# A convolution and a gated scan on one core: the last step's state kept as four plain blocks, the last block's z kept as fp16 halves and summed on TensorE

## The chip, the cores and the metric

The kernel runs on one core of a Trainium2 chip. A core has TensorE (PE in the profile: matmuls from SBUF into PSUM), VectorE (DVE), ScalarE (ACT), GpSimd (POOL) and SyncE (SP), which here issues every DMA of the scan from one queue, in order. The metric is the time of one execution on the device in microseconds, lower is better. An instruction waits on semaphores for what it needs; each engine runs its own instructions in the order in which the program lists them.

## The reference

Input r is 8 sequences of 2048 rows of 512 numbers. Two layers follow each other, both with a residual sum:

```python
x = r
x = x + LN(gelu(irfft(rfft(LN(x)) * Kf)))         # a long convolution over the 2048 rows, its kernel K made from S4 parameters
# second layer: x has shape (8, 2048, 512); axis 0 is the time of the recurrence, 2048 is its batch
c = broadcast(in_c)
for xt in LN(x):                                   # 8 steps
    f = sigmoid(xt @ wf.T + c @ uf.T + bf)
    i = sigmoid(xt @ wi.T + c @ ui.T + bi)
    g = tanh(xt @ wc.T + c @ uc.T + bc)
    c = f * c + i * g
h = tanh(LN(x) @ wo.T + c_final @ uo.T + bo)       # for every step, with the last state
out = x + LN(h)
```

So an output row of any step can only be finished when the last state c_final of its batch row is known.

## The kernel before, in words

**Stages.** The first 690 us or so compute the set-up and the convolution. From there to about 2790 us runs the scan, and the last 80 us finish output rows. The 2048 batch rows are worked in four blocks q of 512 (`NQB` = 4), each of four chunks of 128 rows (`QC` = 4); for every block the eight steps t are run one after the other (`NB` = 8), 32 steps in all, about 66 us each. Matrix products are made with fp16 pairs: a number is a high half plus a low half, and a product takes three matmuls (hi x hi, lo x hi, hi x lo; `mm3`). All values under a tanh or sigmoid are scaled by `SW` on the way.

**A step.** It has eight units: two z units (z0, z1: the part LN(x) @ wo.T of the output, for half of the block's rows each) and six gate units g0 to g5 (three gates, two halves). A unit multiplies 2 x 2 blocks by seven products in place of eight, so its operands are seven combinations of blocks (`xf`, `cf`, the weights). `part_a` issues the first products into a PSUM tile `u` (pool `pu`, three tiles that turn over), then ScalarE copies a quarter of it out (L988) and VectorE makes four additions (L989 to L992). `part_b` issues the remaining products; a gate unit then goes to ScalarE's tanh (L1016) and, with its unit's last gate, to `state`; a z unit is copied to SBUF by ScalarE (L1002, L1003, tile `zt`) beside the quarter `zc`, which VectorE's chain had made, and three DMAs store both to `z_d` in fp32.

On TensorE the units overlap: part_a of the next unit stands ahead of part_b of the one before. The start of a step is part_a(z0), the rest of the step before, part_a(z1), part_b(z0), part_a(g0), part_a(g1), part_b(z1), part_b(g0) and so on. With three tiles, g1 uses the tile of z0 and g2 that of z1.

**The state.** `state` makes the new c (`cd`, four blocks of 128 x 256) on VectorE, L1034 to L1037, three sums of blocks on VectorE (L1040 to L1042), and then `halves` splits seven blocks, the four plain and the three sums, into fp16 pairs `cf`: four ScalarE copies (L1049) and four VectorE subtractions (L1051). For the first half of the state, `halves` is run later.

**Other work in the scan** is placed by hand: `put(list of functions, base, positions)` files small pieces under a position (16 positions a step), and `go(p)` issues those of position p. The main ones are `turn` (LN and the seven combinations of the next step's x), `prep` (last pieces of the convolution's rows), and `head`: during block q the output rows of block q-1 are finished, one at a time; z is read from `z_d` (tile `zr`), GpSimd adds the state's part `ur` (L1123), ScalarE makes the tanh (L1126), VectorE the statistics (L462 to L465), GpSimd the power (L471) and the signs (L475, L476), ScalarE the norm (L1140), and GpSimd adds x (L1141).

**The state's part of the output**, c_final @ uo.T + bo, is made by `last(q)` at the boundary of a block: `load` (weights `uw`), `load_b` (the bias bo), and per chunk `sums` (matmuls L450 to L452 over blocks of `cf`, some of them the sums' blocks) and `out` (ScalarE copies the PSUM tile, GpSimd adds the bias, L1100), then `store` to `u_d`.

**The last block** has no block after it, so its 32 tiles of 128 x 512 (four chunks by eight steps) are finished behind the scan by `tail`, in 16 pairs of tiles; such a pair is called a row below. The first nine rows' z are loaded before the scan ends. A row goes through `load` (z from `z_d`), `load_x`, `sum_` (two VectorE adds of the state's part in PSUM, L1174, and two tanh on ScalarE, L1175), `stat` (VectorE and GpSimd), `norm` (ScalarE, L1182), `out` (x + norm: GpSimd, L1187, one in eight of them on VectorE) and `store` (L1190). A loop issues the stages of several rows interleaved, by offsets:

```python
for st_, d in ((0, -3), (1, -3), (6, 5), (2, 1), (3, 2), (4, 3), (5, 3)):
```

Nine z tiles and nine x tiles turn over, so that x of row n + 9 can be loaded when the store of row n has landed; SP's queue has both, in order.

Of the kernel before, what the change touches and what calls it, by code (L numbers as in the profile page):

```python
# [19 lines left out]
P = 128  # L20
L = 2048
H = 512
# [37 lines left out]
def s4_gated_block(ctx, tc, a, dbg=None):  # L60
# [10 lines left out]
    x1_d = dram.tile([NJ, P, NB, H], F32, name="x1_d")  # L71
    z_d = dram.tile([NJ, P, NB, H], F32, name="z_d")
    u_d = dram.tile([NJ, P, H], F32, name="u_d")
    wf_d = dram.tile([7, P, 2, 7, 2, BP], F16, name="wf_d")
# [379 lines left out]

    def lnstat(src, tag):

        n = len(src)
        st = FE.tile([P, n, 6], F32, name="st" + tag)
        mv = FE.tile([P, n, 2], F32, name="mv" + tag, bufs=2)
        rs = FE.tile([P, n], F32, name="rs" + tag, bufs=2)  # L460
        for i, v in enumerate(src):
            V.bn_stats(st[:, i], v)  # L462
        for i in range(n):
            V.bn_aggr(mv[:, i], st[:, i])
        V.tensor_scalar(rs, mv[:, :, 1], EPS, None, ALU.add)  # L465
        return n, mv, rs, tag
# [527 lines left out]
    def part_b(key):  # L994
# [3 lines left out]
        wx, wc = views(key)  # L998
        mms(u, places(key, THEN), *wx, False, z or not t)
        if z:  # L1000
            zt, zc = FT.tile([P, 3, BP], F32, name="zt"), gates["z"]
# [23 lines left out]
    def state(q, t, n):  # L1025
# [5 lines left out]
        for h in range(2):  # L1031
            hs = slice(2 * h, 2 * h + 2)
            if t == 0:
                V.tensor_scalar(f[:, hs], f[:, hs], 1.0, c0d[:, n + 2 * h : n + 2 * h + 1], ALU.add, ALU.mult)  # L1034
            else:
                V.scalar_tensor_tensor(f[:, hs], f[:, hs], 1.0, cd[:, hs], ALU.add, ALU.mult)  # L1036
            V.scalar_tensor_tensor(cd[:, hs], f[:, hs], 0.5, ig[:, hs], ALU.mult, ALU.add)  # L1037

        ts = f
# [17 lines left out]
    def last(q):  # L1057
# [14 lines left out]

        def load_b():
            bo = FE.tile([P, H], F32, name="bo", tag="xa", bufs=2) if end else FT.tile([P, H], F32, name="bo", tag="x1r", bufs=2)
            dma(out=bo, in_=a["bo"])
            uws.append(bo)

        def sums(cj):
# [5 lines left out]
            us[cj] = u  # L1084
            ps = [(k, b) for k in ((0, 2, 1, 3) if end else range(KT)) for b in (((FB11,) if i == 0 else (FB11, FT1)) if k < 2 else ((FB21,) if i == 0 else (FB22,)))]
            for n, (k, b) in enumerate(ps):
                mm3(u[:, cj % 2], lambda l: cf[k % 2][:, b, l, cs], lambda l: uws[k][:, l],
                    start=(n == 0), stop=(n == len(ps) - 1))

        def out(cj):  # L1090
            p_ = us[cj][:, cj % 2]
            if end:
                V.scalar_tensor_tensor(p_, uws[KT], SW, p_, ALU.mult, ALU.add)
                us_[QC * q + cj] = p_
            else:
                u_ = FT.tile([P, H], F32, name="u_", tag="zr", bufs=4)
                S.activation(u_, p_, AF.Copy)
                if cj == 0:
                    S.mul(uws[KT], uws[KT], SW)
                Q.tensor_tensor(u_, u_, uws[KT], ALU.add)  # L1100
                uo.append(u_)
# [6 lines left out]
        each = [one(f, cj) for cj in range(QC) for f in (sums, out)]  # L1108
        return [load, load_b] + (each[::2] + each[1::2] if end else each + [store])

# [37 lines left out]
    def tail(q, cj, tp, n):  # L1148
# [3 lines left out]
        def load():  # L1152
# [3 lines left out]
            s_["z"] = tails[w][:, n % 3]  # L1156
            dma(out=s_["z"], in_=z_d[c, :, 2 * tp : 2 * tp + 2])

# [12 lines left out]
        def sum_():  # L1171
            for i in range(2):
                z = s_["z"][:, i]
                V.tensor_tensor(z, z, us_[c], ALU.add)  # L1174
                S.activation(z, z, AF.Tanh, scale=1.0 / SW)  # L1175

        def stat():
            s_["s"] = lnscale(lnstat([s_["z"][:, i] for i in range(2)], "h"))

# [4 lines left out]
        def out():  # L1184
            for i in range(2):
                z, x = s_["z"][:, i], s_["x"][:, i]
                (V if n % 4 == 3 and i else Q).tensor_tensor(x, x, z, ALU.add)  # L1187

        def store():
            dma(out=a["out"][c, :, 2 * tp : 2 * tp + 2], in_=s_["x"])  # L1190

        return load, load_x, sum_, stat, norm, out, store

    tails = {}
    gsc = (0.5 / SW, 0.5 / SW, 1.0 / SW)
    bias = FE.tile([P, 3, KT], F32, name="bias")
# [26 lines left out]
    for n, (q, t) in enumerate(steps):  # L1223

        if n > 1 and t:
            when += [(n, p) for p in (at_(5, 10, 15) if t in (2, 3) or n == 4 else at_(5, 10) if t == NB - 1 else (PA, PB))]
    end = last(NQB - 1)
    rows = [tail(NQB - 1, cj, tp, 4 * cj + tp) for cj in range(QC) for tp in range(NB // 2)]

# [5 lines left out]
    for n, (q, t) in enumerate(steps):  # L1235
# [5 lines left out]
        if q and t == 0:  # L1241
            put(last(q - 1), b, (-1, 4, 3, 5, 5, 7, 7, 9, 13, 14, 15))
        if n == len(steps) - 1:
            put(end[:2], b, (2, 3))
            for i in range(3):
# [11 lines left out]
    with tc.manual_schedule(engines=MAN | {mybir.EngineType.SP}):  # L1257
# [25 lines left out]
        for p in sorted(todo):  # L1283
            go(p)
        for f in end[2:6]:
            f()
        for n in range(len(rows) + 5):
            if n % 4 == 0 and n < len(rows):
                end[6 + n // 4]()
            for st_, d in ((0, -3), (1, -3), (6, 5), (2, 1), (3, 2), (4, 3), (5, 3)):  # L1290
                if 0 <= n - d < len(rows) and (st_ > 1 or n - d > (2 if st_ else 8)):
                    rows[n - d][st_]()

_CONSTS = {}
# [60 lines left out]
```

## Time and profile before

| what | value |
|---|---|
| time, median of 3 runs | 2872.67 us (2871.69 to 2873.89) |
| the profiled execution: span from first to last instruction | 2869.6 us |
| what lies around the span (median less span) | 3.1 us |
| mean granted TensorE clock | 0.966 of full speed |
| TensorE / VectorE / ScalarE / GpSimd busy | 89% / 73% / 52% / 42% of the span |
| step length in the scan where nothing waits | 65.94 us |
| stretch from 2802 us to the end | 67.6 us: VectorE 57.0, GpSimd 54.0, ScalarE 42.0, TensorE 5.9 us busy |

How to read it: an answer of the trace has the start in microseconds, the duration, the engine, the line of the kernel and the operation with its tiles; a bracket tells how long the engine stood idle before it and what ended that. A group xN is N instructions in a row. Lines are those of the kernel before. The profile is of one execution; its times are compared with each other, and the sum of a prediction is carried over to the median with the 3.1 us.

### The profile page before, as it was taken

How to read it: one execution, taken by the hardware profiler on the slowest of the kernel's cores; microseconds unless marked ns; L12 is line 12 of the kernel's file. 1: busy time of each engine (PE TensorE's matmuls, PEld its weight loads, DVE VectorE, ACT ScalarE, POOL GpSimd, SP SyncE). 2: the span in 40 equal slices, each digit the busy share in tenths (PEclk: the TensorE clock that was granted, in tenths of full speed). 3: DMA queues.
4: the chain of work that ended last, by engine and by line, in shares of the span. 5: the costliest groups of instructions: out<-in, count | busy, mean ns of one | idle time of the engine just before them, and what ended most of it. 6: DMA issues, size and time to landing. Idle time of an engine off the chain costs nothing.

```text
span 2869.6 us, 60008 instructions
## 1 busy us (share of the span) xinstructions
PE 2567.3 (89%) x23940; PEld 2236.0 (78%) x23940; DVE 2097.3 (73%) x4248; ACT 1478.7 (52%) x3091; POOL 1213.1 (42%) x1496
## 2 busy tenths in 40 slices
PE   4588888876999999999999998999999999999991
PEld 3377777765888888778888886888888788888880
DVE  7878788837667766677777777777777677776758
ACT  8966666634344444445455544455454445544435
POOL 5776777613112221114554531355444124443317
PEclk8799999987999999999999999999999999999995
DMA  6978887797324333224565532355564235543356
GB/s 232 312 233 261 254 263 247 243 263 204 112 65 115 103 93 92 78 89 138 152 174 151 141 100 89 106 161 165 147 163 140 85 89 152 151 130 100 89 163 244
DMA packets 521937, 451.10 MB, mean 157 GB/s; under 512 B 289974, under 2 KB 401080, under 8 KB 516664
## 3 DMA queue, kind: packets, MB, share of 16 engines
q1 hardware_dynamic: 521224, 446.74, 52.4%
q8 instruction: 187, 3.06, 0.4%
q14 instruction: 94, 0.77, 0.1%
q10 hardware_dynamic: 432, 0.52, 0.1%
HBM read 295.41 MB, written 151.78 MB: 156 GB/s over the span
## 4 chain that ended last, share of the span: by engine, by line
PE 34%; DVE 9%; ACT 3%; DMA 2%; issue 1%; POOL 1%; SPq 0%; POOLq 0%; ACTq 0%; DVEq 0%
PE u L950 32%; PE pt L485 1%; DVE u L992 1%; DVE gate L1036 1%; DVE cf L1051 1%; DMA z_d<-zc 1%; ACT xf L101 1%; DVE cd L1037 1%; ACT gate L1016 1%; DVE sth L462 1%; DVE zz L1174 1%; DVE sty L462 1%; ACT y L903 0%; DVE u2p L989 0%; DVE xf L102 0%
## 5 line engine op out<-in xcount | busy, mean ns | idle before, releaser
L950 PEld LDWEIGHTS <-w 128*128 128x128 f16 x15120 | 1482.5, 98 | 217.2 <-issue 28.3
L950 PE MATMUL u<-xf,w 128*128 128x256 f16 x8064 | 947.6, 274 | 30.7 <-ACT zt L1003 12.7
L950 PE MATMUL u<-cf,w 128*128 128x256 f16 x7056 | 826.2, 273 | 3.8 <-DVE cf L1051 3.8
L988 ACT ACTIVATE u2p<-u 128x256 f32<-128x256 f32 x256 | 96.4, 378 | 449.8 <-PE u L950 449.6
L950 PE MATMUL u<-w,xf 128*128 128x256 f16 x2688 | 314.4, 275 | 14.8 <-DVE u L992 4.8
L989 DVE TENSOR_TENSOR u2p<-u2p,u 128x256 f32<-128x256 f32 x256 | 106.8, 417 | 285.8 <-ACT u2p L988 284.3
L1141 POOL TENSOR_TENSOR x1r<-x1r,zr 128x512 f32<-128x512 f32 x96 | 132.7, 1382 | 426.8 <-ACT zr L1140 309.4
L1016 ACT ACTIVATE gate<-u,bias 128x512 f32<-128x512 f32 (+1 forms) x384 | 200.5, 574 | 217.0 <-PE u L950 217.0
L950 PEld LDWEIGHTS <-xf 128*128 128x128 f16 x2688 | 264.6, 99 | 49.5 <-issue 10.7
L904 POOL TENSOR_TENSOR xr<-y,xr 128x512 f32<-128x512 f32 x120 | 160.4, 1357 | 308.2 <-ACT y L903 308.2
L992 DVE TENSOR_TENSOR u<-u,u2p 128x512 f32<-128x512 f32 x256 | 179.0, 699 | 8.8
L647 POOL TENSOR_TENSOR u<-xg,u 128x512 f16<-128x512 f32 x104 | 128.8, 1242 | 114.0 <-ACT u L645 113.9
L471 POOL TENSOR_TENSOR rsy<-rsy,nhalf 128x2 f32<-128x2 f32 (+1 forms) x68 | 50.9, 748 | 296.7 <-DVE rsy L465 284.4
L641 POOL TENSOR_TENSOR xg<-xg,mu 128x512 f32<-128x512 f32 x112 | 162.7, 1459 | 6.0 <-DMA xg<-in_xr 6.0
L102 DVE TENSOR_TENSOR x<-pxt,x 128x256 f16<-128x256 f32 x240 | 100.0, 418 | 63.2 <-ACT x L101 62.3
L1123 POOL TENSOR_TENSOR zr<-zr,ur 128x512 f32<-128x512 f32 x96 | 129.7, 1351 | 22.4 <-DMA zr<-z_d 16.6
L1021 DVE SCALAR_TENSOR_TENSOR gate<-gate,gate 128x1024 f32<-128x1024 f32 x64 | 93.4, 1459 | 59.8 <-ACT gate L1016 59.0
L462 DVE BATCH_NORM_STATS2 sty<-y 128x6 f32<-128x512 f32 x120 | 76.7, 681 | 72.7 <-DMA y<-y_d 72.7
L101 ACT ACTIVATE x<-pxt 128x256 f16<-128x256 f32 x240 | 91.5, 382 | 74.1 <-PE pxt L667 68.4
L101 ACT ACTIVATE xf<-pt 128x512 f16<-128x512 f32 x124 | 60.7, 489 | 133.4 <-DVE xf L102 114.4
L667 PE MATMUL pxt<-x,at 128*128 128x256 f16 x224 | 61.8, 276 | 75.1 <-DVE x L102 73.9
L450 PE MATMUL pyt<-u,t 128*128 128x128 f16 (+2 forms) x544 | 121.4, 223 | 5.4 <-ACT y L746 5.4
(371 smaller groups left out, 5319.1 us busy)
## 6 DMA issues: line engine op xcount, KB each, us to landing
xs<-in_rr SPq DMA_DIRECT2D x32, 1024.0 KB, 5.7
t<-kpad SPq DMA_DIRECT2D x32, 1024.0 KB, 5.6
y_d<-y SPq DMA_DIRECT2D x30, 1024.0 KB, 7.6
xr<-in_r SPq DMA_DIRECT2D x60, 512.0 KB, 5.5
xa<-x_d SPq DMA_DIRECT2D x120, 256.0 KB, 4.1
y<-y_d SPq DMA_DIRECT2D x59, 512.0 KB, 5.7
x_d<-xr SPq DMA_DIRECT2D x59, 512.0 KB, 3.2
xg<-in_xr SPq DMA_DIRECT2D x28, 1024.0 KB, 8.7
```

Of the source, the lines that this page charges most:

```text
L101: S.activation(hi, src, AF.Copy)
L450: T.matmul(out, lhsT=w(0), rhs=x(0), start=start, stop=False)
L462: V.bn_stats(st[:, i], v)
L641: Q.tensor_tensor(xg, xg, bc(mu1), ALU.subtract)
L647: (V if g == 2 else Q).tensor_tensor(u[:, js, 1], xg, u[:, js, 0], ALU.subtract)
L904: Q.tensor_tensor(xv, yv, xv, ALU.add)
L950: T.matmul(u[:, d], lhsT=w(f, b, i == 1, k), rhs=x(f, b, i == 2, k), start=opens and bank not in seen, stop=stop and j == len(n) - 1, skip ...
L989: V.tensor_tensor(u2, u2, u[:, UY], ALU.add)
L992: V.tensor_tensor(u[:, 2:4], u[:, 2:4], u2[:, None].to_broadcast([P, 2, BP]), ALU.add)
L1016: act = lambda o, s_, b: S.activation(o, s_, AF.Tanh, scale=gsc[kind], bias=b)
L1123: Q.tensor_tensor(s_["z"], s_["z"], us_[c], ALU.add)
L1141: Q.tensor_tensor(s_["x"], s_["x"], s_["z"], ALU.add)
```

## The change

Four things are changed.

1. **The state at step 7** is not split into seven blocks but into its four plain ones: `state` leaves out L1040 to L1042 and makes two copies and two subtractions, for both halves at once. `sums` therefore uses the four plain blocks: 12 matmuls in each chunk, plus two for the bias (identity `id16` times the bias's halves `bo16`), so that GpSimd's bias adds fall away. The halves are made once, in `load_bo`, at position 34 (in the third step).
2. **z units of the last block** are stored as fp16 pairs: ScalarE makes three high halves (L1005), VectorE three low halves by subtraction (L1007), two of them from the PSUM tile and one from `zc`, and two DMAs store the tile `zh` to `zl_d`. The bytes are the same as before.
3. **In the tail** `sum_` is made on TensorE: `zacc` adds the two halves of z (identity times z, four matmuls of 512 columns for a row) into a PSUM tile, `sum_` adds the halves `u16` of the state's part (four more), and ScalarE takes the tanh from PSUM. `split` makes `u16` once per chunk.
4. **In the tail** the `EPS` addition (L465) goes from VectorE to GpSimd, and the last addition is one on GpSimd and one on VectorE for every row. The order of the loop is changed for the new stage 7 (`zacc`).

The instructions of the convolution keep their order on every engine. New tiles `u16`, `bo16` and `id16` (about 10 KB a partition) shift the places of the other tiles of their pool.

```diff
--- before.py
+++ after.py
@@ -70,6 +70,7 @@
 
+    zl_d = dram.tile([QC, P, NB, 2, 2, BP], F16, name="zl_d")
     u_d = dram.tile([NJ, P, H], F32, name="u_d")
     wf_d = dram.tile([7, P, 2, 7, 2, BP], F16, name="wf_d")
     uo_d = dram.tile([KT, P, 2, H], F16, name="uo_d")
@@ -452,7 +453,7 @@
         T.matmul(out, lhsT=w(0), rhs=x(1), start=False, stop=stop)
 
 
-    def lnstat(src, tag):
+    def lnstat(src, tag, eps=True):
 
         n = len(src)
         st = FE.tile([P, n, 6], F32, name="st" + tag)
@@ -462,7 +463,7 @@
             V.bn_stats(st[:, i], v)
         for i in range(n):
             V.bn_aggr(mv[:, i], st[:, i])
-        V.tensor_scalar(rs, mv[:, :, 1], EPS, None, ALU.add)
+        (V if eps else Q).tensor_scalar(rs, mv[:, :, 1], EPS, None, ALU.add)
         return n, mv, rs, tag
 
     def lnscale(s_, neg=True):
@@ -997,6 +998,19 @@
         u, z = units.pop(key), kind == "z"
         wx, wc = views(key)
         mms(u, places(key, THEN), *wx, False, z or not t)
+        if z and q == NQB - 1:
+            zh, zc = FT.tile([P, 4, 2, BP], F16, name="zh", tag="zt"), gates["z"]
+            parts = ((0, u[:, UX]), (slice(1, 3), u[:, 2:4]), (3, zc[:, n]))
+            for ds, v in parts:
+                S.activation(zh[:, ds, 0], v, AF.Copy)
+            for ds, v in parts:
+                V.tensor_tensor(zh[:, ds, 1], v, zh[:, ds, 0], ALU.subtract)
+
+            def store():
+                for i in range(2):
+                    dma(out=zl_d[n + 2 * i, :, t], in_=zh[:, 2 * i : 2 * i + 2])
+
+            return store
         if z:
             zt, zc = FT.tile([P, 3, BP], F32, name="zt"), gates["z"]
             S.activation(zt[:, 0], u[:, UX], AF.Copy)
@@ -1035,6 +1049,16 @@
             else:
                 V.scalar_tensor_tensor(f[:, hs], f[:, hs], 1.0, cd[:, hs], ALU.add, ALU.mult)
             V.scalar_tensor_tensor(cd[:, hs], f[:, hs], 0.5, ig[:, hs], ALU.mult, ALU.add)
+            if t == NB - 1:
+                if h == 0:
+                    cf = FT.tile([P, 4, 2, BP], F16, name=f"cf{n}", bufs=2 - n)
+                    cfs.setdefault((q, t), []).append(cf)
+                S.activation(cf[:, hs, 0], cd[:, hs], AF.Copy)
+        if t == NB - 1:
+            for h in range(2):
+                hs = slice(2 * h, 2 * h + 2)
+                V.tensor_tensor(cf[:, hs, 1], cd[:, hs], cf[:, hs, 0], ALU.subtract)
+            return
 
         ts = f
         V.tensor_tensor(ts[:, 0:2], cd[:, 1:3], cd[:, 0:2], ALU.subtract)
@@ -1070,11 +1094,6 @@
                 dma(out=u2, in_=uo_d[2 * i : 2 * i + 2].rearrange("k p a m -> p k a m"))
                 uws.extend(u2[:, k] for k in range(2))
 
-        def load_b():
-            bo = FE.tile([P, H], F32, name="bo", tag="xa", bufs=2) if end else FT.tile([P, H], F32, name="bo", tag="x1r", bufs=2)
-            dma(out=bo, in_=a["bo"])
-            uws.append(bo)
-
         def sums(cj):
             cf, i, cs = cfs[q, NB - 1], cj // 2, slice(cj % 2 * P, (cj % 2 + 1) * P)
             if end and cj % 2:
@@ -1082,22 +1101,19 @@
             else:
                 u = pu.tile([P, 4, BP], F32, name="u").rearrange("p (a b) c -> p a (b c)", a=2)
             us[cj] = u
-            ps = [(k, b) for k in ((0, 2, 1, 3) if end else range(KT)) for b in (((FB11,) if i == 0 else (FB11, FT1)) if k < 2 else ((FB21,) if i == 0 else (FB22,)))]
-            for n, (k, b) in enumerate(ps):
-                mm3(u[:, cj % 2], lambda l: cf[k % 2][:, b, l, cs], lambda l: uws[k][:, l],
-                    start=(n == 0), stop=(n == len(ps) - 1))
+            for l in range(2):
+                T.matmul(u[:, cj % 2], lhsT=id16, rhs=bo16[:, l], start=(l == 0), stop=False)
+            for k in (0, 2, 1, 3):
+                b = ((0, 3), (1, 2))[i][k // 2]
+                mm3(u[:, cj % 2], lambda l: cf[k % 2][:, b, l, cs], lambda l: uws[k][:, l], start=False, stop=(k == 3))
 
         def out(cj):
             p_ = us[cj][:, cj % 2]
             if end:
-                V.scalar_tensor_tensor(p_, uws[KT], SW, p_, ALU.mult, ALU.add)
-                us_[QC * q + cj] = p_
+                split(u16[:, cj, 0], u16[:, cj, 1], p_)
             else:
                 u_ = FT.tile([P, H], F32, name="u_", tag="zr", bufs=4)
                 S.activation(u_, p_, AF.Copy)
-                if cj == 0:
-                    S.mul(uws[KT], uws[KT], SW)
-                Q.tensor_tensor(u_, u_, uws[KT], ALU.add)
                 uo.append(u_)
 
         def store():
@@ -1106,7 +1122,7 @@
 
         one = lambda f, cj: lambda: f(cj)
         each = [one(f, cj) for cj in range(QC) for f in (sums, out)]
-        return [load, load_b] + (each[::2] + each[1::2] if end else each + [store])
+        return [load] + (each[::2] + each[1::2] if end else each + [store])
 
     def head(q, cj, t):
 
@@ -1154,7 +1170,14 @@
             if n % 3 == 0:
                 tails[w] = (FW if w < 2 else FV if w == 2 else FT).tile([P, 3, 2, H], F32, name="zz", tag=f"w{w}", bufs=1)
             s_["z"] = tails[w][:, n % 3]
-            dma(out=s_["z"], in_=z_d[c, :, 2 * tp : 2 * tp + 2])
+            s_["h"] = s_["z"].bitcast(F16).rearrange("p i (a l b) -> p i a l b", a=2, l=2)
+            dma(out=s_["h"], in_=zl_d[cj, :, 2 * tp : 2 * tp + 2])
+
+        def zacc():
+            s_["p"] = pu.tile([P, 4, BP], F32, name="u").rearrange("p (i a) b -> p i a b", i=2)
+            for i in range(2):
+                for l in range(2):
+                    T.matmul(s_["p"][:, i], lhsT=id16, rhs=s_["h"][:, i, :, l], start=(l == 0), stop=False)
 
         def load_x():
             i = (n + 3) % 9
@@ -1170,12 +1193,13 @@
 
         def sum_():
             for i in range(2):
-                z = s_["z"][:, i]
-                V.tensor_tensor(z, z, us_[c], ALU.add)
-                S.activation(z, z, AF.Tanh, scale=1.0 / SW)
+                for l in range(2):
+                    T.matmul(s_["p"][:, i], lhsT=id16, rhs=u16[:, cj, l].rearrange("p (a b) -> p a b", a=2), start=False, stop=(l == 1))
+            for i in range(2):
+                S.activation(s_["z"][:, i], s_["p"][:, i].rearrange("p a b -> p (a b)"), AF.Tanh, scale=1.0 / SW)
 
         def stat():
-            s_["s"] = lnscale(lnstat([s_["z"][:, i] for i in range(2)], "h"))
+            s_["s"] = lnscale(lnstat([s_["z"][:, i] for i in range(2)], "h", False))
 
         def norm():
             for i, (nm, rs) in enumerate(s_["s"]):
@@ -1184,14 +1208,25 @@
         def out():
             for i in range(2):
                 z, x = s_["z"][:, i], s_["x"][:, i]
-                (V if n % 4 == 3 and i else Q).tensor_tensor(x, x, z, ALU.add)
+                (V if i else Q).tensor_tensor(x, x, z, ALU.add)
 
         def store():
             dma(out=a["out"][c, :, 2 * tp : 2 * tp + 2], in_=s_["x"])
 
-        return load, load_x, sum_, stat, norm, out, store
+        return load, load_x, sum_, stat, norm, out, store, zacc
 
     tails = {}
+    u16 = FT.tile([P, QC, 2, H], F16, name="u16")
+    bo16 = FT.tile([P, 2, H], F16, name="bo16")
+    id16 = FT.tile([P, P], F16, name="id16")
+
+    def load_bo():
+        bo = FT.tile([P, H], F32, name="bo", tag="x1r", bufs=2)
+        dma(out=bo, in_=a["bo"])
+        S.activation(bo16[:, 0], bo, AF.Copy, scale=SW)
+        V.scalar_tensor_tensor(bo16[:, 1], bo, SW, bo16[:, 0], ALU.mult, ALU.subtract)
+        S.activation(id16, ident, AF.Copy)
+
     gsc = (0.5 / SW, 0.5 / SW, 1.0 / SW)
     bias = FE.tile([P, 3, KT], F32, name="bias")
     bias0 = FE.tile([P, 3, KT], F32, name="bias0")
@@ -1224,6 +1259,7 @@
 
         if n > 1 and t:
             when += [(n, p) for p in (at_(5, 10, 15) if t in (2, 3) or n == 4 else at_(5, 10) if t == NB - 1 else (PA, PB))]
+    put([load_bo], 0, (34,))
     end = last(NQB - 1)
     rows = [tail(NQB - 1, cj, tp, 4 * cj + tp) for cj in range(QC) for tp in range(NB // 2)]
 
@@ -1239,9 +1275,9 @@
             for i in range(2):
                 put(turn(*steps[n + 1], i), b, ps[i])
         if q and t == 0:
-            put(last(q - 1), b, (-1, 4, 3, 5, 5, 7, 7, 9, 13, 14, 15))
+            put(last(q - 1), b, (-1, 3, 5, 5, 7, 7, 9, 13, 14, 15))
         if n == len(steps) - 1:
-            put(end[:2], b, (2, 3))
+            put(end[:1], b, (2,))
             for i in range(3):
                 put(rows[i][:2], b, (8 + 2 * i, 9 + 2 * i))
             for i in range(3, 9):
@@ -1282,14 +1318,15 @@
         part_b(before)
         for p in sorted(todo):
             go(p)
-        for f in end[2:6]:
+        rows[0][7]()
+        for f in end[1:5] + [end[5]]:
             f()
         for n in range(len(rows) + 5):
-            if n % 4 == 0 and n < len(rows):
-                end[6 + n // 4]()
-            for st_, d in ((0, -3), (1, -3), (6, 5), (2, 1), (3, 2), (4, 3), (5, 3)):
-                if 0 <= n - d < len(rows) and (st_ > 1 or n - d > (2 if st_ else 8)):
+            for st_, d in ((0, -3), (1, -3), (6, 5), (2, 1), (7, 0), (3, 2), (4, 3), (5, 3)):
+                if 0 <= n - d < len(rows) and (st_ > 1 or n - d > (2 if st_ else 8)) and (st_ < 7 or n):
                     rows[n - d][st_]()
+            if n < 3:
+                end[6 + n]()
 
 _CONSTS = {}
 
@@ -1344,7 +1381,7 @@
     import concourse.bacc as bacc
     from concourse.bass_utils import run_bass_kernel_spmd
 
-    nc = bacc.Bacc("TRN2", target_bir_lowering=False, num_devices=1)
+    nc = bacc.Bacc("TRN2", target_bir_lowering=False, num_devices=1, dynamic_dma_scratch_size=1024)
     arrays = {f"in_{k}": v for k, v in _arrays(inputs).items()}
     a = {k[3:]: nc.dram_tensor(k, v.shape, mybir.dt.from_np(v.dtype), kind="ExternalInput").ap() for k, v in arrays.items()}
     a["out"] = nc.dram_tensor("out", (NJ, P, NB, H), F32, kind="ExternalOutput").ap()
```

## The prediction

> **What bounds the kernel now.** I read the page's busy times and its chain first, then TensorE's waits in the scan, then engine timelines of one step and of the end. On the page:
>
> ```profile
> PE 2567.3 (89%) x23940; PEld 2236.0 (78%) x23940; DVE 2097.3 (73%) x4248; ACT 1478.7 (52%) x3091; POOL 1213.1 (42%) x1496
> PE 34%; DVE 9%; ACT 3%; DMA 2%; issue 1%; POOL 1%; SPq 0%; POOLq 0%; ACTq 0%; DVEq 0%
> ```
>
> TensorE is the bound through the scan; VectorE is second. From 2583 to 2790 us TensorE is busy for 206.89 of 207.00 us, so each microsecond for which it waits there is one more in the time. TensorE's waits from 800 to 2790 us (total, times, longest) are short:
>
> ```profile
> PE u L950 <- ACT zt L1003: 12.7, 11, 3.3
> PE u L450 <- ACT cf L1049: 1.8, 1, 1.8
> PE u L450 <- DMA uw<-uo_d: 0.7, 1, 0.7
> ```
>
> The first line matters most: the PSUM tile `u` of a z unit comes free when ScalarE's copy L1003 has read it, and the change puts VectorE behind that copy. The timelines of step t = 5 of the last block (start, duration, engine, line) show how much time there is:
>
> ```profile
> 2602.88 0.37 ACT L1002 ACTIVATE zt<-u 128x256 f32<-128x256 f32 x1
> 2603.14 0.59 ACT L1003 ACTIVATE zt<-u 128x512 f32<-128x512 f32 x1
> 2604.37 0.70 DVE L992 TENSOR_TENSOR u<-u,u2p 128x512 f32<-128x512 f32 x1
> 2604.98 0.68 DVE L462 BATCH_NORM_STATS2 sth<-zr 128x6 f32<-128x512 f32 x1
> 2604.81 2.78 PE L950 MATMUL u<-xf,w 128*128 128x256 f16 x24
> ```
>
> The copies belong to z unit 0, L992 ends the chain of z unit 1, and the matmuls at 2604.81 are the first of gate unit 1, which reuses z unit 0's tile (three tiles turn over: z0, z1, g0, then g1 in z0's). It was free at 2603.73, 1.08 us early.
>
> At the end of the scan TensorE waits for the state's halves, its clock falls, and the rows then run on VectorE and GpSimd:
>
> ```profile
> 2794.14 0.39 PE L451 MATMUL u<-uw,cf 128*128 128x512 f16 x1 [2.47 <-DVE cf L1051]
> 2794.98 0.61 PE L450 MATMUL u<-uw,cf 128*128 128x512 f16 x1
> 2844.37 1.14 DVE L465 TENSOR_SCALAR rsh<-mvh 128x2 f32<-128x2 f32 x1
> 2843.00 2.48 POOL L1187 TENSOR_TENSOR xx<-xx,zz 128x512 f32<-128x512 f32 x2
> ```
>
> The tiny L465 takes 1.14 us there, until GpSimd's pair of adds is done, against 0.17 at 2852.59. Rows follow each other at 3.84 us (GpSimd's L476 at 2842.82 and 2846.66).
>
> **z of the last block, +13.6 us.** 16 units each gain three VectorE subtractions (0.42, 0.70, 0.42, as L989 to L992 last) and one ScalarE copy (0.4). VectorE is idle for 74 us in 2583 to 2790 (133.0 busy of 207), so the work as such costs nothing; its place does. In each step z0's subtractions stand on VectorE behind the whole chain of z1, and at t = 3 and 6 behind a statistics task too (1.07 us: 2604.98 to 2606.05, where g0's chain starts). The tile is free only after the second, some 0.35 + 0.70 = 1.05 us after the moment D at which VectorE has ended what stands ahead. With N the start of g1's matmuls, from the same timelines: t = 1: D 2330.74, N 2331.63, late by 0.16. t = 2: 2399.34, 2398.14, 2.25. t = 3: 2469.20, 2464.91, 5.34. t = 4: 2537.94, 2534.72, 4.27. t = 5: 2604.98, 2604.81, 1.22. t = 6: 2671.33, 2670.75, 1.63. t = 7: 2737.27, 2736.68, 1.64. At t = 0 no unit is late: z0's tile is asked for after a last-state sum that is itself waited for. Sum 16.5. Of it, waits that stand later in the same steps take back 0.58 (2472.86, on L992) and 2.33 (2548.34, on L1003, whose copy waited 4.08 for stores): 13.6. Behind the waiting matmul stands all of TensorE's queue; behind the subtractions stands g0's chain (L989 at 2606.05), whose result is needed only at about 2612. z1's tile has more room: its copies come after the last product at 2612.0 and g2 wants it 3.9 us later, against 1.0 of copies and 1.1 of subtractions. Bounds: 9 if all the existing waits of these steps, 5.7 in all, are swallowed and some of D comes earlier; 20 if one more statistics task is in front in some steps.
>
> The stores fall from three to two per unit, of the same bytes, behind the subtractions; SP gains one slot of 0.4 us per unit, which bounds nothing. The `zc` tile is released by VectorE rather than by a store (ScalarE waited 7.4 us twice for it); TensorE's only waits near them are 0.41 at 2482.61 and the 2.33 counted above, so I take 0.
>
> **State halves of step 7, -1.5 us.** Per unit VectorE loses L1040 to L1042 and two subtractions (0.7 + 0.43 + 0.42 + 0.42 + 0.68, about 2.5 us), and ScalarE loses two copies. At three block boundaries the cf wait of 1.8 us (2264.73) can go. But the weights `uw` arrive by then too: at 1732.74 the same sum waited 0.73 for them. I take 0.5 each. The later waits of the boundaries (ACT gate 1.1, u_ 3.0) are for other work and stay. Bounds: 0 and 3 x 1.8 = -5.4. The sums fall from 60 to 56 matmuls of 512 columns, 4 x 0.216 = 0.9 per block, while two of these are the bias; that is inside the same 0.5. The bias adds on GpSimd (1.26 to 1.82, 12 of them) and their loads lay beside TensorE: 0.
>
> **Set-up and the first step, 0.** New tiles u16, bo16, id16 shift the layout; by the order of instructions the first gate1 tile's write must now wait for GpSimd's xrb add (until 674.67, where L990 stood at 669.36): VectorE 5.3 us later, in front of a gap of 7.31 (688.30, on DMA x_d<-x1e). And SP no longer waits 22.8 us for that add at L890, so those stores issue earlier. Bounds -3 and +3.
>
> **End and rows, -0.4 us.** Ahead of the wait for cf1 now stand zacc (4) and the bias (2); the halves of cf1 are ready near 2793.4 instead of 2795.9. But all of sums 0 to 3 but the last stay ahead of the first row's four matmuls, so the first tanh comes at about 2804, where it was at 2801.57: +2.4, less the shorter first row on GpSimd (one add of 1.25 instead of 2.48): the first output store +1.2. Per row VectorE loses its adds (1.28) and gains one (0.62), so 1.20 + 0.40 + 0.62 = 2.2; ScalarE stays at 1.23 + 1.50 = 2.73; GpSimd has 0.22 + 0.71 + 0.19 + 0.22 + 1.25 plus gaps, 2.8, and if VectorE's add shuts it out 3.4. So rows could come every 3.4 us instead of 3.84, 7.0 less over 16. They can't all: SP's queue stores a row, waits for its landing, loads x into its place and only then stores the next:
>
> ```profile
> 2839.09 0.32 SPq L1169 DMA_DIRECT2D xx<-x_d  x1
> 2845.49 0.32 SPq L1169 DMA_DIRECT2D xx<-x_d  x1
> ```
>
> One link is 6.4 us there; six links take 34.3 us from the first store (2811.62) to the seventh (2845.91), behind which z of the last row is loaded, and VectorE waited for that z already (0.32 at 2853.09). With the first store 1.2 later, the last row starts 1.2 later; its drain saves 1.2 (half of the adds on VectorE) and 0.4 (TensorE for VectorE). Bounds -7 and +4.
>
> A weighing of two rules. VectorE's final add at 2863.34, beside GpSimd's, took 1.41 us where 0.68 is usual, and GpSimd's 1.71 for 1.25. The Trainium skill ("SBUF — State Buffer", Who interferes with whom) says that a VectorE instruction with two SBUF inputs contends with a GpSimd instruction that reads SBUF and that the later one blocks fully; that speaks against moving one add of each row to VectorE, and by it the row is 3.4 rather than 2.8. On the clock the row is 2794.98: matmuls 0.43 apart after gaps of 1.39 and 2.47 us, 0.216 again from 2797.98. The Trainium skill ("TensorE: Matmul & The Clock Gate", What's actually happening) asks for a busy window of about 3.4 us before full speed; the rows with 1.73 us of matmuls each would then never reach it and take 8 x 0.43 = 3.44 us, as long as the row itself: the sum would stay, with no room left.
>
> **Sum.** 13.6 - 1.5 + 0 - 0.4 = +11.7 on the profiled execution, whose span 2869.6 lies 3.1 below the median 2872.67: 2884.
>
> **Rivals.** A, the rows pay it back: one mechanism, the SP link. If a link falls from 5.7 on average to 3.5 us (z stores of the scan land in 3.3, but 512 KB loads took 6 to 7), the last z no longer holds and the rows run at ScalarE's 2.73: 16 x 1.1 = -17.6 in place of -0.4: 2884 - 17 = 2867, and just faster. It decides from links below about 3.5. Against it: these links carry 1.5 MB each. 0.12. B, a second wait: z1's copies wait until z0's stores have landed (one `zt` buffer), and those are now issued behind the subtractions. At t = 4 such a wait cost TensorE 2.33; if it came in five more steps, +11.7: 2896. It needs landings over 7.4 us, and the median of the stores is 3.3. 0.17. C, the late tile is swallowed: existing waits take 5.7 of the 16.5, boundaries give 5.4 and rows 7: -1.6, 2871, no change. 0.14. My forecast: 0.57.
>
> **Numbers.** Faster or slower count from 0.2%, 5.7 us, which is about what a measurement of this kernel can tell. Range 2867 (A's middle) to 2897 (B's middle): it leaves out half of A and of B and a little of the forecast's own. Faster: A and the end of C, 0.14; same: most of C and the low end of the forecast, 0.14; slower 0.72.
>
> **What would show it.** Right: in the changed profile, TensorE's waits in the last block name VectorE at the zh subtraction, seven times, 13 to 17 us in all; none of these in the first three blocks; the boundary's cf wait replaced by `uw`; output rows' loads still 6 us apart. Wrong: no such wait (the place of the subtractions), or a span from 2800 us to the end that is shorter by over 5 us (the SP link).

## The result, and the profile after

The changed kernel takes 2887.56 us (median of 5 runs, 2883.47 to 2888.55); the kernel before takes 2872.67 in the same comparison (5 runs, 2868.53 to 2874.30). The ratio is 1.0051 (95% interval 1.0039 to 1.0063): slower by 0.5%. The forecast was 2884, with 2867 to 2897 as its range. The profiled execution has a span of 2881.6 us, 12.0 more than before (2869.6); it is the fastest of the five, while the medians lie 14.9 apart, so the stretches below account for 12.0. The median of the kernel before lies between 2870.0 and 2875.4 us in the different sets of runs, so the experiments below are compared by their ratios and, inside a profile, by stretches.

The page of the changed kernel, busy times and the chain that ended last:

```profile
PE 2604.1 (90%) x24052; PEld 2250.2 (78%) x24052; DVE 2080.9 (72%) x4221; ACT 1477.0 (51%) x3094; POOL 1185.4 (41%) x1488
PE 57%; DVE 9%; ACT 4%; issue 2%; POOL 2%; DMA 1%; SPq 0%; ACTq 0%; POOLq 0%; DVEq 0%
```

TensorE has 37 us more of busy time, 34 of it behind the scan, in the sums of the rows; VectorE and GpSimd have less. The busy times alone do not show where the scan lost time. Of TensorE's waits between 800 and 2810 us (total, times, longest) these four lines matter:

```profile
PE u L951 <- DVE zh L1007: 16.6, 8, 5.3
PE u L951 <- ACT zt L1017: 8.2, 8, 2.7
PE u L1105 <- ACT u__30179 L1116: 1.7, 1, 1.7
PE u L452 <- DVE cf L1060: 0.9, 1, 0.9
```

The first line is new: eight waits of a `u` tile for VectorE's subtraction L1007 (the eighth, of 0.2, lies at a boundary of blocks). The old line of waits for ScalarE's `zt` has shrunk from 12.7 to 8.2, mostly as three of those waits, 3.6 us together, lay in the last block. In time order, on TensorE's timeline (start, duration, operation, wait in brackets), the seven are:

```profile
2328.71 2.79 PE L951 MATMUL u<-xf,w 128*128 128x256 f16 x24 [0.27 <-DVE zh L1007]
2397.49 4.33 PE L951 MATMUL u<-xf,w 128*128 128x256 f16 x24 [2.67 <-DVE zh L1007]
...
2471.23 4.99 PE L951 MATMUL u<-xf,w 128*128 128x256 f16 x24 [5.25 <-DVE zh L1007]
2543.58 4.46 PE L951 MATMUL u<-xf,w 128*128 128x256 f16 x24 [4.04 <-DVE zh L1007]
2612.42 2.79 PE L951 MATMUL u<-xf,w 128*128 128x256 f16 x24 [1.07 <-DVE zh L1007]
2680.14 2.79 PE L951 MATMUL u<-xf,w 128*128 128x256 f16 x24 [1.61 <-DVE zh L1007]
2747.74 2.79 PE L951 MATMUL u<-xf,w 128*128 128x256 f16 x24 [1.50 <-DVE zh L1007]
```

One wait in each of the steps 1 to 7. Behind the three longest the same 24 matmuls take 4.3 to 5.0 us in place of 2.79: the clock had fallen (granted clock 0.58 from 2469 to 2477 us, 1.00 in the 8 us behind).

Where the 12.0 us of the two profiled executions lie, by the start of the copy of z0 in the first step, the same copy in step 25 (steps counted from 0, so t = 1 of the last block), the end of the scan's last gate unit, and the span's end. "The last block" stands for its steps t = 1 to 7 from here on:

| stretch | before | after | difference |
|---|---|---|---|
| start to z0 of step 0 | 715.14 | 720.09 | +4.95 |
| from there to z0 of step 25 (three boundaries in it) | 1612.93 | 1604.88 | -8.05 |
| from there to the end of the scan (the last block) | 460.36 | 474.53 | +14.17 |
| end of the scan to the end | 81.17 | 82.10 | +0.93 |

### The profile page after: what moved, and what is told of

Same layout as the page of the kernel before. It is cut to its first block, busy times and chain, and to the rows that moved or that the text cites. A ratio compares the mean times of both kernels' runs of the same rounds, so it can differ in the third digit from the quotient of the medians.

```text
span 2881.6 us, 60255 instructions
## 1 busy us (share of the span) xinstructions
PE 2604.1 (90%) x24052; PEld 2250.2 (78%) x24052; DVE 2080.9 (72%) x4221; ACT 1477.0 (51%) x3094; POOL 1185.4 (41%) x1488
## 4 chain that ended last, share of the span: by engine, by line
PE 57%; DVE 9%; ACT 4%; issue 2%; POOL 2%; DMA 1%; SPq 0%; ACTq 0%; POOLq 0%; DVEq 0%
PE u L951 53%; PE pt L486 2%; DVE u L993 1%; DVE cd L1051 1%; DVE gate L1050 1%; ACT xf L102 1%; ACT gate L1030 1%; DVE cf L1075 1%; DVE u2p L990 1%; DVE xf L103 1%; ACT y L904 0%; DVE sty L463 0%; POOL xr L905 0%; POOL rsh L472 0%; PE u L452 0%
## 5 line engine op out<-in xcount | busy, mean ns | idle before, releaser
L993 DVE TENSOR_TENSOR u<-u,u2p 128x512 f32<-128x512 f32 x256 | 179.0, 699 | 8.7
L472 POOL TENSOR_TENSOR rsx<-rsx,nhalf 128x2 f32<-128x2 f32 (+1 forms) x66 | 52.6, 796 | 261.4 <-DVE rsx L466 260.7
```

The lines of the kernel that those rows point to most:

```text
L993: V.tensor_tensor(u[:, 2:4], u[:, 2:4], u2[:, None].to_broadcast([P, 2, BP]), ALU.add)
```

## The experiments

**place_late: the new tiles get addresses behind the others.** In the changed kernel `u16`, `bo16`, `id16` are the first tiles of their pool, and all others move up, onto a tile that the convolution's last rows still read.

```diff
-    u16 = FT.tile([P, QC, 2, H], F16, name="u16")
-    bo16 = ...; id16 = ...          # ahead of load_bo
     def load_bo():
         bo = FT.tile([P, H], F32, name="bo", tag="x1r", bufs=2)
+        u16 = FT.tile([P, QC, 2, H], F16, name="u16")
+        bo16 = ...; id16 = ...
```

> Edit to the changed kernel: the tiles u16, bo16 and id16 are allocated at position 34 (third step) and so get addresses behind the others, so that gate1 and the first y tile no longer overlap the place of the tile that GpSimd's xrb addition still reads. Nothing else. Theory (the 5.0 us of the first step are the place of the new tiles: VectorE 5.99 and the y load 23.8 us wait for that addition): the wait of gate1 for xrb is gone, the first z0 copy of the scan is back near 715 us (it was 715.14 before the change, 720.09 after), and the time falls by 5, from 2887.6 to about 2882.6. Rival (something else in the set-up, for example the DMA scratch, or the first step is bound by another chain that is as late): copy at 718 to 720 us, time within 2 us of 2887.6.

VectorE's timeline of the changed kernel has, in the first step,

```profile
675.43 0.42 DVE L991 TENSOR_TENSOR gate<-u2p,u 128x256 f32<-128x256 f32 x1 [5.99 <-POOL xrb L554]
```

and SP's queue, after an idle stretch of 23.8 us, the y load that stood at 651.23 before the change:

```profile
675.42 0.62 SPq L881 DMA_DIRECT2D y<-y_d  x1
```

With place_late the wait of `gate` is gone and the y load is back:

```profile
651.39 0.62 SPq L882 DMA_DIRECT2D y<-y_d  x1
```

From VectorE's first addition of the scan to the copy of z0 it was 46.6 us before, 51.4 with the change, 47.2 now; the other four kernels with this edit have 47.0 to 47.7, the other four without it 50.7 to 51.6. So the place is what delays the first step, by some 4 us. (The last line of the change's diff, which sets the DMA scratch, is in place_late too, and so is not the cause.) How much of it reaches the end is less clear: the profile of place_late is 3.9 us ahead of the changed kernel's at z0 of step 0, but only 1.9 at the end of the scan, and the ratio, 1.0046 (1.0029 to 1.0062) against 1.0051, can't tell 5 us from nothing.

**copy_out: the PSUM tile is free after ScalarE.**

```diff
-    zh, zc = FT.tile([P, 4, 2, BP], F16, name="zh", tag="zt"), gates["z"]
-    parts = ((0, u[:, UX]), (slice(1, 3), u[:, 2:4]), (3, zc[:, n]))
+    zh, zc = FT.tile([P, 4, 2, BP], F16, name="zh"), gates["z"]      # a place of its own
+    zt = FT.tile([P, 3, BP], F32, name="zt")
+    S.activation(zt[:, 0], u[:, UX], AF.Copy)
+    S.activation(zt[:, 1:3], u[:, 2:4], AF.Copy)
+    parts = ((0, zt[:, 0]), (slice(1, 3), zt[:, 1:3]), (3, zc[:, n]))
```

> Edit to the changed kernel: in the last block ScalarE copies the z unit's three quarters from PSUM into an fp32 tile, as before the change, and the fp16 halves are made from that tile; so the PSUM tile is free after ScalarE, while VectorE has the same three subtractions in the same place and ScalarE two copies more. Theory (the 14 us of the last block are the PSUM tile that waits for VectorE): TensorE's eight waits on the subtraction (16.6 us) are gone, with the slow matmuls that follow three of them (24 matmuls in 4.3 to 5.0 us in place of 2.78); some older waits come back (0.58, 0.86 and 2.33): time 2887.6 - 14 = 2873 to 2875. Rival (the added work of VectorE and ScalarE, or the stores, cost the time wherever they stand): no change or slower, 2887 to 2890.

2870.28 us; ratio 0.9994 (0.9985 to 1.0003), so 0.57% or 16 us below the changed kernel, 2 more than expected. TensorE's timeline in the last block:

```profile
2393.18 2.78 PE L951 MATMUL u<-xf,w 128*128 128x256 f16 x24 [0.41 <-ACT zt L1005]
2401.78 2.14 PE L951 MATMUL u<-xf,w 128*128 128x256 f16 x18 [1.23 <-DVE u L993]
2459.33 2.23 PE L951 MATMUL u<-cf,w 128*128 128x256 f16 x19 [0.72 <-DVE cf L1078]
2471.71 3.80 PE L951 MATMUL u<-xf,w 128*128 128x256 f16 x18 [2.94 <-DVE u L993]
2540.53 2.14 PE L951 MATMUL u<-xf,w 128*128 128x256 f16 x18 [1.05 <-DVE u L993]
```

None names `zh`, and behind step 4 there is no wait at all. The last block takes 459.8 us: the 14.2 are gone. (`zh` no longer shares the place of `zt`, but the waits that are gone named the subtraction, not a store.) VectorE has as much to do as in the changed kernel, and more: the subtractions now have both inputs in SBUF, and at t = 3 three of them took 4.1 us beside GpSimd, where 2.2 had done mostly from PSUM. VectorE's timeline of copy_out, then of the changed kernel:

```profile
2465.66 2.62 DVE L1010 TENSOR_TENSOR zh<-zt,zh 128x256 f16<-128x256 f32 x2
2468.20 1.48 DVE L1010 TENSOR_TENSOR zh<-zc,zh 128x256 f16<-128x256 f32 x1
```

```profile
2470.15 1.02 DVE L1007 TENSOR_TENSOR zh<-u,zh 128x256 f16<-128x256 f32 x2
2471.09 1.19 DVE L1007 TENSOR_TENSOR zh<-zc,zh 128x256 f16<-128x256 f32 x1
```

Behind these subtractions stands the chain that ends with L993, for which TensorE waits at t = 2 to 4 (1.0 to 2.9). Yet the block is no longer than before the change: it was not the work that cost the time, it was the tile that waited for it.

**subs_first: the subtractions ahead of the next unit's chain.** The tile still waits for VectorE, only the order is changed.

```diff
-    part_a(key)
-    go(p)
+    chain = part_a(key, bool(q == NQB - 1 and t and sl == 1))   # z1 of the last block: additions held back
+    if not chain:
+        go(p)
     ...
         finish(before, p + 1)
+    if chain:
+        chain()
+        go(p)
```

> Edit to the changed kernel: in steps 1 to 7 of the last block z0's subtractions stand on VectorE ahead of z1's chain of four additions (and of the task filed between them) instead of behind it; the PSUM tile still waits for VectorE. Theory (the price of each step is what stands ahead of the subtractions): each release comes 2.0 us sooner (four additions) and 3.1 in the two steps with a statistics task ahead; by the waits of the changed kernel, 0.27, 2.67, 5.25, 4.04, 1.07, 1.61, 1.50 in t = 1 to 7, some 0.6, 2.2 and 2.0 remain at t = 2, 3, 4 and none elsewhere: 9 to 11 us less with the slow matmuls, time 2877 to 2879. Rival (VectorE as a whole is too full, the order is not it): the delayed chain of z1 makes a wait of its own and the time stays at 2885 to 2890.

2874.64 us; ratio 1.0015 (1.0006 to 1.0025), 10 us below the changed kernel, the last block 463.2. Six waits for the subtractions are left; two of them, at t = 2 and t = 3:

```profile
2396.87 2.79 PE L951 MATMUL u<-xf,w 128*128 128x256 f16 x24 [1.47 <-DVE zh L1013]
...
2466.96 4.25 PE L951 MATMUL u<-xf,w 128*128 128x256 f16 x24 [2.93 <-DVE zh L1013]
```

The six are 9.6 us together, not the 4.8 expected: the waits at t = 2 to 4 fell to 1.5, 2.9 and 2.2 (from 2.7, 5.3, 4.0), and z1's subtractions, which the move pushes back, make new ones (0.76, 1.43, 0.78), as the rival had it. The time still falls by the 9 to 11 us expected, as only one of the waits is followed by slow matmuls. The order is a good part of the price, as the theory says; the tile's release by ScalarE is worth more.

**zload_ahead: z of the late rows loaded nine rows ahead.**

```diff
-for st_, d in ((0, -3), (1, -3), ...
+for st_, d in ((0, -9), (1, -3), ...
```

> Edit to the changed kernel: the loads of z of rows 9 to 15 are issued nine rows ahead instead of three, so that they no longer stand behind the links of store, landing and x load in SP's queue. Theory (the last rows wait for SP's links): TensorE's 10.7 us of waits for z in the tail are gone; then GpSimd's row of 3.43 us sets the end: its 16 rows from 2819 end near 2872 in place of 2876, so 3 to 5 us less: 2883 to 2884.5. Rival (the transfers themselves are the limit, or x of the late rows arrives late too): the waits move to the x tiles, the time stays at 2886 to 2888.

Ratio 1.0039 (1.0024 to 1.0054), by itself hardly told from 1.0051. From the end of the scan to the end it takes 78.3 us in place of 82.1: 3.8 less, as expected (the kernels without this edit that leave the tail as it is have 81.8 to 82.9). No matmul waits for z any more, and GpSimd's rows go on at one pace to the last. Its timeline, one power for each row:

```profile
2864.73 1.24 POOL L472 TENSOR_TENSOR rsh<-rsh,nhalf 128x2 f32<-128x2 f32 x1
2868.17 1.24 POOL L472 TENSOR_TENSOR rsh<-rsh,nhalf 128x2 f32<-128x2 f32 x1
2871.61 1.24 POOL L472 TENSOR_TENSOR rsh<-rsh,nhalf 128x2 f32<-128x2 f32 x1
```

3.44 us a row, and the power is 1.24 us long where it is 0.72 when VectorE makes no addition beside it. The x loads stay 5.5 to 7.3 us apart; z no longer stands behind them.

**state_alone: the kernel before with the state's four blocks and the bias on TensorE, without the rest.** `z`, its stores and the tail are as before.

> The kernel before with one part of the change alone: step 7's state as four plain blocks and the bias as two matmuls (its tiles allocated late, as in place_late); z, its stores and the tail are as before the change, VectorE's bias addition at the end falls away. Theory (the boundaries gain about 1.9 us each by the shifts of the step starts, +4.94 to +3.05, +0.51 to -1.37, -1.41 to -3.29, and the last block loses nothing): three times 1.9 and 1 to 2 at the end of the scan, 6 to 8 less than before: 2864 to 2866. Rival (the shifts at the boundaries are drift between two executions): within 2 us of before.

Ratio 0.9972 (0.9959 to 0.9985): faster than the kernel before, by 8.0 us, the upper end of what was expected. The steps from 7 to 9, 15 to 17 and 23 to 25, with a boundary in each, are 2.0, 1.3 and 2.7 us shorter (in the changed kernel 1.8, 2.6, 1.7), the last block 0.5, and from the end of the scan to the end 77.4 us in place of 81.2. There the wait for the second half of the state is

```profile
2791.71 0.39 PE L452 MATMUL u<-uw,cf 128*128 128x512 f16 x1 [0.88 <-DVE cf L1048]
```

where it was 2.47 before; the clock does not fall, and the first tanh comes 9.5 us after the end of the scan (13.1 before, 15.7 in the changed kernel). So one part of the change gains 8 us, and the rest, z in halves with its tail and the place of the new tiles, loses more than 20 as it stands. The second number is the difference of the two ratios; the rest was not run by itself.

**three_mended: place_late, copy_out and zload_ahead in one kernel.**

> The changed kernel with the three edits place_late, copy_out and zload_ahead together. Theory (three separate costs): the gains add, 2887.6 - 4 - 17 - 4 = 2862 to 2863, 9 us below the kernel before. Rival (one of them hides behind another: with z loaded ahead the rows still end with GpSimd, and the first step's delay is taken up by waits of the boundaries): 2866 to 2870.

2867.67 us, ratio 0.9968 (0.9957 to 0.9979): 9.2 below the kernel before, the 9 that were expected. Within these intervals the three costs add. It is also not to be told from state_alone (0.9972): mended, z in halves with the sums on TensorE is worth about nothing, give or take some 4 us.

**vector_adds: both final additions on VectorE, x two rows ahead.**

```diff
-((0, -9), (1, -3), ...
+((0, -9), (1, -2), ...
-(V if i else Q).tensor_tensor(x, x, z, ALU.add)
+V.tensor_tensor(x, x, z, ALU.add)
```

> three_mended, and in the tail both final additions of a row on VectorE (GpSimd keeps only the five small operations) and x loaded two rows ahead instead of three, so that an x load waits for a store issued two links earlier. Theory (GpSimd's row of 3.44 us, in which its power takes 1.24 instead of 0.72 beside VectorE's addition, sets the tail): VectorE then has 1.2 + 0.3 + 1.25 = 2.8 and ScalarE 2.7 per row: 16 rows 0.6 shorter each, -8 to -10 against three_mended, about 2853 to 2855. Rival (VectorE's additions wait for ScalarE's norm and stand ahead of the next row's statistics, a loop through VectorE, GpSimd and ScalarE): rows of 3.4 to 4 us, no gain or a loss of up to 8.

2857.69 us; ratio 0.9942 (0.9924 to 0.9960), 16.7 below the kernel before and 7.5 below three_mended. This is a little under the 8 to 10 expected. GpSimd's powers of every other row:

```profile
2816.73 1.01 POOL L472 TENSOR_TENSOR rsh<-rsh,nhalf 128x2 f32<-128x2 f32 x1
...
2822.77 1.01 POOL L472 TENSOR_TENSOR rsh<-rsh,nhalf 128x2 f32<-128x2 f32 x1
...
2828.82 1.01 POOL L472 TENSOR_TENSOR rsh<-rsh,nhalf 128x2 f32<-128x2 f32 x1
```

6.05 us for two rows, 3.02 each, where 2.8 was expected; in the rows between, the power takes 0.72. From 2802 to 2849 us VectorE is busy for 42.0 of 47.0 (29.3 in three_mended) and GpSimd for 27.2 (37.3). GpSimd now waits for VectorE in every row (1.48 and 0.41 us by turns), so it no longer sets the pace. The end of the scan to the end takes 71.8 us. The edit holds two changes, the additions and the x loads, and they were not run apart.

**row0_first: one chunk's sums ahead of the first row.**

```diff
-for f in end[1:5] + [end[5]]:
+for f in (end[1], end[5]):
     f()
 ...
-    if n < 3:
-        end[6 + n]()
+    if 1 <= n < 4:
+        end[1 + n]()
+        end[5 + n]()
```

> Edit to the changed kernel: behind the scan only the first chunk's sums and split stand ahead of the first row; the other three chunks' sums and splits (2.6 us of TensorE each) are issued after rows 0, 1 and 2. Theory (the first row waits for all four sums, and the last row's z for the SP chain that begins with the first store): the first tanh comes some 7.8 us sooner after the scan, the first store about as much, z of the last row 5 to 7 sooner, so the stretch from the end of the scan to the end falls from 82.1 to 75 to 77 us and the time from 2887.6 to 2881 to 2883. Rival (TensorE, with 1.7 us of its own in each row and 2.6 of sums between them, delays rows 1 to 3, and the rest catches up): first tanh sooner, end within 2 us of the changed kernel.

Here the theory fell. The first tanh does come 8.0 us after the end of the scan in place of 15.7; but the second row's power comes 4.7 us after the first's (2.0 in the changed kernel), the first store only 2.4 us sooner, and the stretch to the end is 80.5 us, 1.6 less. Ratio 1.0040 (1.0025 to 1.0055), not to be told from 1.0051. The rival (the rest catches up, an end within 2 us) holds.

**all_mended: vector_adds with that edit.**

> vector_adds with the edit of row0_first: placement late, PSUM copied out by ScalarE, z loaded nine rows and x two rows ahead, both final additions on VectorE, and the first row ahead of the other chunks' sums. Theory (nothing but the rows' own engines then holds the tail, 3.0 us a row): the start 7.8 us sooner less some 3 us for sums between the rows: 4 to 6 below vector_adds, which was 16.7 below the kernel before, so 0.992 to 0.993 of the time before. Rival (the start was hidden behind the loads of x and z): no gain against vector_adds, 0.994.

Ratio 0.9942 (0.9926 to 0.9959), the same as vector_adds; the end takes 71.2 us against 71.8. The rival holds in its outcome; what takes the head start back, sums between the rows or the loads, I did not separate.

## Why the prediction was right

The largest term, its cause and its place were right. That the sum, +11.7, came within 0.3 us of the profiled +12.0 was luck beyond that: the state gained 6.5 us more than its term, and the first step (4.95), the end (1.3) and z (0.6) cost 6.9 more than theirs. The medians lie 14.9 apart, where 11.3 was forecast.

**z of the last block, +13.6: right, by two misses that cancel.** The waits by the table of D and N were 0.16, 2.25, 5.34, 4.27, 1.22, 1.63, 1.64, together 16.5; the profile has 0.27, 2.67, 5.25, 4.04, 1.07, 1.61, 1.50, together 16.4. Reading the time at which VectorE is done with what stands ahead, and the time at which the tile is wanted, from the old trace gave each wait to within 0.45 us. The term that corrects for old waits was too small: 2.9 taken back, while the block's old waits fell from 6.1 to 0.7. And a term was missing: the slow matmuls behind the long waits, 1.5 + 2.2 + 1.7 = 5.4 us, against 1.7 for one such place before. 16.4 - 5.4 + 3.7 = 14.7, measured 14.2. The slow matmuls are in part chance: in row0_first the wait at t = 2 is 2.67 again, the 24 matmuls behind it take 2.79, and the block is 1.5 us shorter. copy_out shows that the tile is the cause and subs_first that the order sets the price.

**State halves, -1.5: the sign right, the size a quarter of the truth.** The whole stretch gave 8.05, beyond the bound of 5.4; the three boundaries gave 6.1 of it. The step that failed is "inside the same 0.5": I folded the four matmuls that each boundary saves into the gain of the cf wait. They are a gain of their own, 4 x 0.216 = 0.9 for each, beside the waits of 0.3, 0.7 and 1.8, since TensorE is the bound there: 5.5 of the 6.1. The `uw` wait that I set against it did not come. The remaining 2 of the 8.05 lie inside blocks 1 and 2; there these kernels differ from one execution to another by as much (zload_ahead, with the same code there, stood 3.3 us behind the changed kernel at step 15 and 2.3 behind at step 23), so I give them no cause.

**First step, 0: wrong, +4.95, outside its bounds of 3.** The row was the right one (VectorE 5.3 us later, behind the xrb addition), the step after it wrong: "those stores issue earlier". SP's wait for that addition did not go, it moved one DMA forward, from the xr load at 674.70 to the y load at 675.42, and everything behind it in SP's queue followed: the first x1e store from 683.19 to 687.90, and with it VectorE's gap at 688.30.

**End and rows, -0.4: +0.9.** The parts were well sized: first tanh +2.4 (2.5 measured), rows 3.4 us (3.43), first store +1.2 (1.6), z of the last row bound by SP's links of 6 (its load 0.4 us later, counted from the end of the scan; x loads follow each other at 5.7 to 6.1). TensorE's timeline shows the rows stopped by it:

```profile
2835.87 1.02 PE L1180 MATMUL u<-zz,id 128*128 128x512 f16 x4 [1.55 <-ACT zz L1199]
...
2846.55 1.86 PE L1180 MATMUL u<-zz,id 128*128 128x512 f16 x4 [3.25 <-DMA zz<-zl_d]
...
2864.49 1.52 PE L1180 MATMUL u<-zz,id 128*128 128x512 f16 x4 [2.78 <-DMA zz<-zl_d]
2865.81 1.91 PE L1197 MATMUL u<-u,id 128*128 128x512 f16 x4
```

The mis-sized term is the drain, "0.4 (TensorE for VectorE)": by then most matmuls run at half speed, and the last row's eight take 3.2 us from the arrival of z where VectorE's two additions took 1.3. From that arrival to the end it was 16.5 us before and is 17.1, not 1.6 shorter.

**The two rules.** On the port the rows are held at another place than in the row I used. Both additions keep their length, 0.69 on VectorE and 1.27 on GpSimd; it is GpSimd's tiny power, which starts 0.03 us behind VectorE's addition, that takes 1.24. In a late row without an addition beside it the power takes 0.71:

```profile
2828.02 0.69 DVE L1211 TENSOR_TENSOR xx<-xx,zz 128x512 f32<-128x512 f32 x1 [1.33 <-ACT zz L1206]
2828.05 1.24 POOL L472 TENSOR_TENSOR rsh<-rsh,nhalf 128x2 f32<-128x2 f32 x1
...
2829.83 1.27 POOL L1211 TENSOR_TENSOR xx<-xx,zz 128x512 f32<-128x512 f32 x1
...
2862.38 0.71 POOL L472 TENSOR_TENSOR rsh<-rsh,nhalf 128x2 f32<-128x2 f32 x1
```

These 0.5 us are most of what lies between a row of 2.8 and one of 3.43. The Trainium skill ("SBUF — State Buffer", Who interferes with whom) lets a VectorE instruction with two SBUF inputs contend with a GpSimd instruction that reads SBUF, and these rows agree with it.

On the clock my reading failed. In the changed kernel's rows 8 to 10, with pauses of 1.55 us, the matmuls were busy for 1.73 of 3.43 us and ran at 0.216 apart all the same (1.02 and 1.03 for four; in rows 1 to 6 they stand without a pause). In zload_ahead eight rows in a row do so, with a granted clock of 1.00 from 2829 to 2857 us. In the changed kernel they fell to half only in the row in front of which TensorE waited 2.58 for z, and the last four rows, with waits of 2.1 to 3.3, stayed there but for a few matmuls (granted clock 0.58 from 2846 to 2868 us). The Trainium skill ("TensorE: Matmul & The Clock Gate", What's actually happening) ties the clock to windows of about 3.4 us, idle or busy; here rows that were half busy kept the full clock, and waits shorter than such a window lost it.

**Rivals.** A (the links pay it back) needs links below 3.5; they were 5.5 on average. With z out of the way alone (zload_ahead) they stay at 5.5 to 7.3; with x a row later too (vector_adds) one link of 6.5 is left, and then the x loads follow each other at 3 to 4 us (2821.19, 2825.25, 2828.45, 2832.22). B (stores held back) did not occur. C's swallowing did (5.4 of 5.7), the slow matmuls undid it.

## What to carry to other kernels

Before handing a PSUM tile's last read to another engine, write down two times for each use from the old trace: when that engine is done with what stands ahead in its order, and when the tile is wanted again; the difference is the wait, and a spare copy by the engine that is early may be cheaper than that wait (here 16 us). Price each part of a change by itself: here one part gained 8 us and the rest lost more than 20, and only running that part by itself showed that it was worth keeping. New tiles at the head of a pool move all others, and a tile that lands on memory still being read delays what is queued behind it (here the first step, by some 4 us).

## What the runs showed of the hardware that I had not expected

- A wait of TensorE can cost more than its length: behind waits of 2.67, 5.25 and 4.04 us the next 24 matmuls took 4.33, 4.99 and 4.46 us instead of 2.78. In the eleven profiles of this case, from 800 us on, none of the 90 waits of 0.2 to 2.21 us in front of 24 such matmuls had this price, 44 of the 57 from 2.27 to 3.32 us had it, and all 8 of 4 us and more. One without it, in the kernel before:

```profile
2014.71 2.78 PE L950 MATMUL u<-xf,w 128*128 128x256 f16 x24 [3.32 <-ACT zt L1003]
```

- Work that fills half of the time kept TensorE at full clock (1.73 of 3.43 us, matmuls 0.216 apart, eight rows in zload_ahead), with pauses of 1.55 us; in the changed kernel, with pauses of 2.1 to 3.3 us, it fell to half and for the most part stayed there.
- GpSimd's power on 128 x 2 numbers takes 0.72 us alone and 1.24 beside a VectorE addition with both inputs in SBUF; VectorE's subtractions of 256 to 512 columns took 4.1 us for three from SBUF beside GpSimd's additions and 2.2 for the same three mostly from PSUM.
